# A graph layer on one core: VectorE adds messages and squares for two groups in one instruction

## The chip, the core and the metric

The kernel runs on one core of a Trainium2 chip. A core has five engines with a queue each: TensorE (PE in the profile, with its weight loads as PEld), VectorE (DVE), ScalarE (ACT), GpSimd (POOL) and SyncE (SP), which here only issues DMAs. Engines run side by side and wait for each other by semaphores; each works through its own queue in order. SBUF is the working memory with 128 partitions, PSUM holds the results of TensorE in eight banks of 2 KB a partition.

The metric is the device time of one execution in microseconds (us). A change is judged by the median of several runs.

## The reference

A graph has 12,500 nodes with 96 features, 412,500 edges sorted by their end node `dst`, and 4 features an edge. Cut to what matters:

```python
def _mlp(h, W, b, gamma, beta):
    h = relu(h @ W + b)
    mu, var = mean(h, 0), mean(square(h - mu), 0)     # over all rows
    return gamma * (h - mu) * rsqrt(var + 1e-5) + beta

node = _mlp(x, W_node, b_node, ...)
edge = _mlp(edge_attr, W_edge, b_edge, ...)
message = concatenate([x[src], x[dst], edge], axis=1)  # 412500 x 288
message = _mlp(message, W_msg, b_msg, ...)
agg = segment_sum(message, dst, num_segments=12500)
out = layernorm(x + agg + node)
```

The message needs the sum and the sum of squares of relu(...) over all edges, so its normalisation is applied at the end, to the sums by node.

## The kernel before

`W_msg` has three parts, and so has the message before its relu. The part of `x[src]` is computed once for all nodes into a table in HBM (`p_tab`, function `tables`), and rows are fetched from there by edge. The part of `x[dst]` lies in a second table (`q_tab`); since edges are sorted by `dst`, a block of edges needs only a window of its rows. The part of the edge is computed anew by TensorE from the edge's features.

**Tiles.** 128 edges are a tile, 4 tiles a group (806 groups), 4 groups a block (202 blocks). The rows of `x[src]` for a group come by `gather` (L210): one indirect DMA of GpSimd for each tile. Groups of the first 29 blocks are gathered early, before their messages can be computed, and put into HBM (`spill`); the main loop gets them back with plain DMAs (`fetch`, tile `pb`). All other groups land in `ring`, which has room for 16 groups, two groups to a tile. In the main loop `ahead_of` issues the gathers of the group 16 places ahead.

**Tiles without a gather.** For some groups the last of the four tiles isn't gathered. `COPIED` (L85) lists 349 such groups: their 128 columns of the transposed `x`, which lies in SBUF as `big`, are copied one by one to a tile `xc` by ScalarE (one column an instruction, L676) or VectorE (two columns an instruction, L672, and one XOR in `mend`, L681, at the end), and TensorE multiplies them by the weights (L779). `LOADS` (L74) says how many columns each of the two copies in each of four successive steps. `BY_ROW` lists 36 groups whose last tile is fetched row by row by SyncE's DMAs.

**The main loop** (`fast`, L867) has one step for each group `k`, in an order of every engine written out by hand (`manual_schedule`). In a step:

- SyncE loads edge features, the window of `q_tab` and numbers for the copies (`load`, `fetch`, `listed`, `fetch_rows`).
- VectorE: a part of the column copies, then `message(k)` (L797): z in PSUM plus the gathered rows, clamped at 0 from below, into a half of `h`. Then more copies, and `moments` (L816): the square of a group, made by ScalarE, is added to `wide_sq`, which lies in the PSUM tile `mixed`. Once a block `places_of` (L805) compares `rel` with `nodes_of`, also in `mixed`, to make the matrix that says which edge belongs to which node, and `add` (L845, L846) adds the finished block's sums to `agg`.
- ScalarE: `squared` (L811) once for two groups, `prepare` (L766: relu of the edge part into `left`) once for two groups, and column copies.
- TensorE: `sums(k - 2)` (L826: sums by node), `linear(k + 2)` (L774, L779: edge part, `x[dst]` part and copied tiles into the next z), `edges` (L758).
- GpSimd: the gathers of a group, always 16 groups ahead.

z has three banks (`ZB` = 3), `h` three tiles of two groups, `left` two tiles of a block, and the PSUM tile `pr` of two banks is used for `edges` and for products that nobody reads (`unread`, L634), which stand at the end between the last sums.

**The end.** After the last group, the last moments, sums and `add`s give mean and variance. `output` (L1103) forms the matrix `d` from them (L1111 to L1118, with two more unread products, L1121), multiplies it with `agg` for 98 tiles of 128 nodes (L1129), and for each eight of these adds the rest (L1135), squares and sums (L1139 or L1141 and L1142), takes root and reciprocal, scales (L1146) and stores. In `output`, groups of eight tiles with odd number are squared by eight ScalarE instructions that also sum, the others by one ScalarE instruction and a sum on VectorE. `general`, for inputs whose windows don't fit, isn't run.

Of the kernel before, what the change touches and what calls it, by code (L numbers as in the profile page):

```python
# [13 lines left out]
F32 = mybir.dt.float32  # L14
# [52 lines left out]
AB, HP, RB, ZB = 2, 3, 3, 3  # L67
# [6 lines left out]
LOADS = (((24,), (28,)) * 2, ((16, 16),) * 4)  # L74
AHEAD_BY = 18
LP = (NG - SPILL) // 2
BUSY = 5
# [7 lines left out]
COPIED = sorted([*range(RING + 1, 2 * (LP - 6), 2), *range(RING + 32, 2 * (LP - 8), 36)])  # L85
# [29 lines left out]
def gnn(ctx, tc, t):  # L115
# [396 lines left out]
    def fast():  # L512
# [49 lines left out]
        with tc.tile_pool(name="fix", bufs=1) as fix, tc.tile_pool(name="msg", bufs=2) as work, \  # L562
# [22 lines left out]
            left = [fix.tile([P, BG, GE], F32, name=f"left{i}") for i in range(2)]  # L585
# [12 lines left out]
            zb = [ps.tile([P, GE], F32, name=f"z{i}", bufs=1) for i in range(ZB)]  # L598

            eas, block, prs, windows = {}, {}, {}, {}  # L600
# [22 lines left out]
            def fetch(s):  # L623
                b = order[s]
                if b * BG < SPILL:
                    back = work.tile([P, BG, GT, C], F32, name="pb", bufs=1)
                    nc.sync.dma_start(back, spill[b].rearrange("p g (a c) -> p g a c", a=GT))
                    for i in range(BG):
                        got[b * BG + i] = back[:, i, :, :]

            def unread(n):
                busy = ps.tile([P, 2, GE], F32, name="pr", bufs=1)[:, 0, :GE // 2]
                for i in range(n):
                    nc.tensor.matmul(busy, ident[:C], big[:C, -GE // 2:], start=True, stop=True)  # L634
# [9 lines left out]
            numbers = [fix.tile([1, TURN, P], I32, name=f"numbers{i}") for i in range(2)]  # L644
# [116 lines left out]
            def prepare(s, half):  # L761

                n = min(2, NG - order[s] * BG - 2 * half)
                if n > 0:
                    pr, x = prs.pop((s, half)), left[s % 2]
                    nc.scalar.activation(x[:, 2 * half:2 * half + n, :], pr[:, :n, :], AF.Relu)  # L766

            def linear(k):
# [4 lines left out]
                for i in range(n):  # L773
                    nc.tensor.matmul(zb[k % ZB][:, i * C:(i + 1) * C],  # L774
                                     left[s % 2][:KR, g % BG, i * P:(i + 1) * P],
# [12 lines left out]
            def message(k):  # L788
                s, g = steps[k]
                n = min(GT, NT - g * GT)  # L790
                z = zb[k % ZB][:, :n * C].rearrange("p (t c) -> p t c", c=C)
                h = hb[k // 2 % HP][:, k % 2, :, :C]
                rows = got.pop(g)
# [3 lines left out]
                nc.vector._custom_dve(TENSOR_ADD_SAT, out=h[:, :n, :], in0=z, in1=rows[:, :n, :],  # L797
# [422 lines left out]
```

## Time and profile before

| | |
|---|---|
| median of 3 runs | 3613.63 us (3613.0 to 3615.57) |
| the profiled execution | 3611.83 us, of which the span from first to last instruction is 3610.1 us |
| mean granted TensorE clock | 0.771 of full speed |
| first message (L795/L797) | at about 612 us of the span |
| last gather begins | at 3545.8 us of the span |
| output products (L1129) | 3557.6 to 3599.8 us |
| VectorE, `moments` | 804 instructions, 444.3 us |
| ScalarE, column copies | 19968 instructions, 1932.9 us |

Times in the views count from the start of the span. A group of instructions is told as: line, engine, operation, out<-in, shapes, count | busy us, mean ns of one | idle time of the engine just before them, and what ended it. Instructions of one engine can overlap at their ends, so busy time divided by count can be less than the mean of one. "issue" is time in which an engine waited for nothing that the profile shows. PEld is TensorE's loading of weights beside its products (PE). Every fp32 product stands in the profile as two instructions.

### The profile page before, as it was taken

The page shows a single profiled execution, that of the slowest core. Times are in us where ns is not written, and L with a number is a line of the kernel's source. Part 1 is how long each engine was busy: PE and PEld are TensorE (multiplying, and loading weights), DVE is VectorE, ACT ScalarE, POOL GpSimd, SP SyncE. Part 2 cuts the span into 40 slices and gives each one's busy share as a digit, 9 for nine tenths or more (in the row PEclk, how much of TensorE's full clock was granted, in tenths as well). Part 3 has the DMA queues.
Part 4 walks back from the last instruction along what each step waited for, and adds up shares of the span by engine and source line. Part 5 has one row for each costly group of instructions (what it writes and reads, how often), then busy time and mean ns, then how long its engine had stood idle before and what let it go on. Part 6 is the DMA issues. An engine that isn't in the chain of part 4 may idle for free. (4 is left out here: it accounts for less than half of the span.)

```text
span 3610.1 us, 90270 instructions
## 1 busy us (share of the span) xinstructions
PE 2588.0 (72%) x15924; PEld 2197.9 (61%) x16147; DVE 3133.6 (87%) x15669; ACT 2989.8 (83%) x21332; POOL 2693.5 (75%) x2853
## 2 busy tenths in 40 slices
PE   4766765787877777776777777767777677777667
PEld 4313412676766666666666666666667566667667
DVE  3798798898988999998999999898999989999843
ACT  1687687788999999888998898899898989889832
POOL 7777777777777777777777777777777777777774
PEclk7766667888788778787877778787887978777875
DMA  9676664222222222222222222222222222222232
GB/s 254 168 199 190 178 191 110 59 64 63 59 64 63 63 60 53 63 63 62 59 65 63 62 64 59 62 64 63 59 64 62 58 60 59 62 63 63 62 99 68
DMA packets 219742, 303.63 MB, mean 84 GB/s; under 512 B 130416, under 2 KB 145894, under 8 KB 219026
## 3 DMA queue, kind: packets, MB, share of 16 engines
q0 software_dynamic: 90720, 139.53, 18.9%
q1 hardware_dynamic: 115474, 153.30, 14.2%
q10 hardware_dynamic: 12960, 4.93, 0.5%
q14 instruction: 459, 3.76, 0.3%
q8 instruction: 129, 2.11, 0.2%
HBM read 241.43 MB, written 56.09 MB: 82 GB/s over the span
## 5 line engine op out<-in xcount | busy, mean ns | idle before, releaser
L215 POOL DMA_INDIRECT pg<-p_tab,src x2771 | 2615.8, 944 | 847.8 <-issue 699.6
L676 ACT ACTIVATE xc<-big 96x1 f32 x19968 | 1932.9, 187 | 116.5 <-issue 102.2
L672 DVE SCALAR_TENSOR_TENSOR xc<-first_of_two,big 96x2 int32<-96x2 int32 x12352 | 1758.1, 209 | 107.8 <-issue 95.4
L774 PE MATMUL z<-rhs,left 128*128 128x96 f32 x6446 | 1137.9, 331 | 649.8 <-DVE h L797 637.5
L774 PEld LDWEIGHTS z<-rhs,left 128*128 128x128 f32 x6446 | 1004.7, 237 | 742.3 <-DVE h L797 729.9
L826 PEld LDWEIGHTS pa<-at,h 128*97 128x97 f32 x6446 | 833.4, 206 | 106.8 <-issue 40.1
L826 PE MATMUL pa<-at,h 128*97 128x80 f32 x6446 | 847.9, 287 | 20.4 <-issue 9.9
L797 DVE CUSTOM_DVE_ANT_0 h<-z,pg 128x384 f32<-128x384 f32 x690 | 377.1, 546 | 198.6 <-DMA pg<-p_tab,src 196.8
L811 ACT ACTIVATE sq<-h 128x768 f32<-128x768 f32 x404 | 335.2, 830 | 212.5 <-DVE mixed L816 204.6
L816 DVE TENSOR_TENSOR mixed<-mixed,sq 128x384 f32<-128x384 f32 x804 | 444.3, 553 | 0.4
L766 ACT ACTIVATE left<-pr 128x1024 f32<-128x1024 f32 x403 | 403.7, 1002 | 35.1 <-PE pr L758 25.1
L446 ACT ACTIVATE r<-pr 128x1024 f32<-128x1024 f32 x303 | 304.0, 1025 | 87.5 <-DVE estats L448 36.7
L448 DVE BATCH_NORM_STATS2 estats<-r 128x6 f32<-128x512 f32 x606 | 363.8, 677 | 8.5 <-ACT r L446 8.5
L442 PE MATMUL pr<-ea,wide 128*128 128x512 bf16 x587 | 249.6, 522 | 118.3 <-ACT r L446 117.8
L758 PE MATMUL pr<-late,we 128*128 128x512 bf16 x515 | 213.0, 474 | 89.1 <-DMA late<-stack 43.4
L442 PEld LDWEIGHTS <-wide 128*128 128x128 bf16 x606 | 71.1, 118 | 279.2 <-issue 265.0
L758 PEld LDWEIGHTS <-we 128*128 128x128 bf16 x806 | 101.4, 132 | 122.6 <-issue 100.9
L779 PE MATMUL z<-w_msg,xc 96*128 96x96 f32 x698 | 157.4, 313 | 0.0
L805 DVE TENSOR_TENSOR at<-rel,mixed 128x496 f32<-128x496 bf16 x202 | 132.0, 653 | 0.0
L779 PEld LDWEIGHTS z<-w_msg,xc 96*128 96x128 f32 x698 | 127.9, 228 | 0.0
L215 POOL DMA_INDIRECT pg<-in_x,src_raw x64 | 60.7, 949 | 20.8 <-issue 19.2
L410 PE MATMUL pn<-scaled,agg 96*128 96x96 f32 x196 | 52.4, 362 | 21.3 <-DVE y0s L413 21.3
(153 smaller groups left out, 1005.9 us busy)
## 6 DMA issues: line engine op xcount, KB each, us to landing
row<-p_tab SPq DMA_DIRECT2D x4608, 0.4 KB
pg<-p_tab,src POOLq DMA_INDIRECT x2771
pb<-spill SPq DMA_DIRECT2D x29, 768.0 KB
spill<-pg SPq DMA_DIRECT2D x55, 384.0 KB
ea<-stack SPq DMA_DIRECT2D x28, 420.0 KB
stack<-y SPq DMA_DIRECT2D x48, 224.0 KB
late<-stack SPq DMA_DIRECT2D x53, 180.0 KB
rhs<-q_tab SPq DMA_DIRECT2D x202, 46.5 KB
```

Source lines behind the costliest of these rows:

```text
L215: made = [nc.gpsimd.indirect_dma_start(out=pg[:, i, :], out_offset=None, in_=tab[:, :], in_offset=bass.IndirectOffsetOnAxis(ap=idx[:, i:i ...
L442: nc.tensor.matmul(pr[:, k % 2, :], wide[:, P * i:P * (i + 1)], ea[:, b % J, :], start=True, stop=True)
L448: nc.vector.bn_stats(stats[:, (k - o) % NS, (k - o) // NS, :], r[:, 1 - o, :])
L672: nc.vector.scalar_tensor_tensor(to[:, lo + i:lo + i + 2], first_of_two, a, b.to_broadcast([C, 2]), op0=OP.bitwise_and, op1=OP.bitwise_xor)
L676: nc.scalar.activation(to[:, lo + i:lo + i + 1], x.bitcast(F32), AF.Copy)
L758: nc.tensor.matmul(prs[s, half][:, i, :], we[:, 2 * half + i, :], block[s], start=True, stop=True)
L766: nc.scalar.activation(x[:, 2 * half:2 * half + n, :], pr[:, :n, :], AF.Relu)
L774: nc.tensor.matmul(zb[k % ZB][:, i * C:(i + 1) * C], left[s % 2][:KR, g % BG, i * P:(i + 1) * P], rhs[:KR, s % RB, g % BG, :], start=True, ...
L797: nc.vector._custom_dve(TENSOR_ADD_SAT, out=h[:, :n, :], in0=z, in1=rows[:, :n, :], s0=MOST, s1=0.0)
L811: nc.scalar.activation(sq[:, :m, :n, :], hb[k // 2 % HP][:, k % 2:k % 2 + m, :n, :C], AF.Square)
L816: nc.vector.tensor_tensor(wide_sq, wide_sq, sq[:, i, :, :], op=OP.add)
L826: nc.tensor.matmul(by_place[s % 2][:C + 1, :NW], hb[k // 2 % HP][:r, k % 2, t, :], at[s % AB][:r, i, o + NW * t:o + NW * (t + 1)], start=i ...
```

## The change

- `ZB` is 4. z lies in two PSUM tiles of two banks each, and `message` handles two groups in one instruction, in even steps; `linear` works three steps ahead.
- `wide_sq` has room for two groups and lies in SBUF; `moments` adds the squares of both groups in one instruction, in odd steps, from the square made in the step before it (`now`; it was one pair older). `nodes_of` is the SBUF tile `iota`. The PSUM tile `mixed` is gone. `places_of` of the next block comes in the third step of a block instead of the fourth.
- `left` has three tiles of half a block instead of two of a block. `numbers` lies in a partition of `big` that held nothing.
- `COPIED` has 366 groups, 17 more; `LOADS` changes from 104 + 128 columns in four steps (ScalarE + VectorE) to 108 + 136.
- `unread` multiplies bf16 tiles (`we`, `rel`) with 512 columns instead of fp32 with 256; there are four such products at each of the three places at the end (before: 4, 3 and 3), and three in each of the last seven steps where no `edges` product is waiting in `pr`.
- `output`: TensorE's order is by hand, the two unread products are bf16 with 512 columns, and eight single squares are used for every third set of tiles (i % 3 == 1) instead of every second.

```diff
-AB, HP, RB, ZB = 2, 3, 3, 3
+AB, HP, RB, ZB = 2, 3, 3, 4
...
-LOADS = (((24,), (28,)) * 2, ((16, 16),) * 4)
+LOADS = (((28,), (24,), (28,), (28,)), ((16, 16), (16, 20)) * 2)
...
-BUSY = 5
+BUSY, WARM, DENSE = 4, 7, 3
...
-COPIED = sorted([*range(RING + 1, 2 * (LP - 6), 2), *range(RING + 32, 2 * (LP - 8), 36)])
+COPIED = sorted([*range(RING + 1, 2 * (LP - 6), 2), *range(RING + 32, 2 * (LP - 8), 18)])
...
-            mixed = ps.tile([P, GE], F32, name="mixed", bufs=1)
-            wide_sq = mixed[:, :GT * C].rearrange("p (t c) -> p t c", c=C)
+            wide_sq = fix.tile([P, 2, GT, C], F32, name="wide_sq")
...
-            nodes_of = mixed[:, GT * C:GT * C + BG * WN].rearrange("p (k w) -> p k w", w=WN)
-            nc.vector.tensor_copy(nodes_of, iota)
+            nodes_of = iota
...
-            left = [fix.tile([P, BG, GE], F32, name=f"left{i}") for i in range(2)]
+            left = [fix.tile([P, 2, GE], F32, name=f"left{i}") for i in range(3)]
...
-            zb = [ps.tile([P, GE], F32, name=f"z{i}", bufs=1) for i in range(ZB)]
+            zp = [ps.tile([P, 2, GE], F32, name=f"z{i}", bufs=1) for i in range(ZB // 2)]
+            zb = [zp[i // 2][:, i % 2, :] for i in range(ZB)]
...
             def unread(n):
-                busy = ps.tile([P, 2, GE], F32, name="pr", bufs=1)[:, 0, :GE // 2]
+                busy = ps.tile([P, 2, GE], F32, name="pr", bufs=1)[:, 0, :]
                 for i in range(n):
-                    nc.tensor.matmul(busy, ident[:C], big[:C, -GE // 2:], start=True, stop=True)
+                    nc.tensor.matmul(busy, we[:, i % BG, :], rel.rearrange("p g t -> p (g t)")[:, :GE], start=True, stop=True)
...
-            numbers = [fix.tile([1, TURN, P], I32, name=f"numbers{i}") for i in range(2)]
+            numbers = [big[C:C + 1, i * TURN * P:(i + 1) * TURN * P].bitcast(I32).rearrange("o (k e) -> o k e", k=TURN) for i in range(2)]
...
-            def message(k):
+            def message(k, m=2):
+
                 s, g = steps[k]
                 n = min(GT, NT - g * GT)
-                z = zb[k % ZB][:, :n * C].rearrange("p (t c) -> p t c", c=C)
-                h = hb[k // 2 % HP][:, k % 2, :, :C]
-                rows = got.pop(g)
+                i = k % 2
+                z = zp[k // 2 % 2][:, i:i + m, :n * C].rearrange("p g (t c) -> p g t c", c=C)
+                h = hb[k // 2 % HP][:, i:i + m, :n, :C]
...
-                nc.vector._custom_dve(TENSOR_ADD_SAT, out=h[:, :n, :], in0=z, in1=rows[:, :n, :],
-                                      s0=MOST, s1=0.0)
+                rows = backs[s][:, g % BG - i:] if g < SPILL else ring[(g - SPILL) % RING // 2]
+                nc.vector._custom_dve(TENSOR_ADD_SAT, out=h, in0=z, in1=rows[:, i:i + m, :n, :], s0=MOST, s1=0.0)
...
-            def moments(sq, i):
-
-                nc.vector.tensor_tensor(wide_sq, wide_sq, sq[:, i, :, :], op=OP.add)
+            def moments(sq, m=2):
+
+                nc.vector.tensor_tensor(wide_sq[:, :m], wide_sq[:, :m], sq[:, :m], op=OP.add)
...
-                    message(k)
+                    if k % 2 == 0:
+                        message(k)
                     j = k - LATER - BG - 1
                     if k % 2 == 0 and k >= 2:
-                        now, before = squared(k - 2), now
+                        now = squared(k - 2)
                         acts.load()
-                    if g % BG == 3 and s + 1 < len(order):
+                    if g % BG == 2 and s + 1 < len(order):
                         places_of(s + 1)
                     dves.load()
                     dves.copy()
-                    if k >= 4:
-                        moments(before, k % 2)
+                    if k % 2 and now is not None:
+                        moments(now)
...
+                    if k >= last - WARM and not prs:
+                        unread(DENSE)
                     acts.copy()
...
-                unread(BUSY - 1)
+                unread(BUSY)
...
-                unread(BUSY - 2)
+                unread(BUSY)
...
-                if i % 2:
+                if i % 3 == 1:
                     for g in range(n):
                         nc.scalar.activation(sq[:, g, :], y[:, g, :], AF.Square, accum_out=sd[:, g:g + 1])
```

More of the change, by code (lines that the diff above doesn't have):

```diff
@@ L627, in fetch @@
                     nc.sync.dma_start(back, spill[b].rearrange("p g (a c) -> p g a c", a=GT))
+                    backs[s] = back
                     for i in range(BG):
@@ L764, in prepare @@
                 if n > 0:
-                    pr, x = prs.pop((s, half)), left[s % 2]
-                    nc.scalar.activation(x[:, 2 * half:2 * half + n, :], pr[:, :n, :], AF.Relu)
+                    pr, x = prs.pop((s, half)), left[(2 * s + half) % 3]
+                    nc.scalar.activation(x[:, :n, :], pr[:, :n, :], AF.Relu)
             def linear(k):
@@ L865, in fast @@
                 places_of(0)
-                now, before, last = None, None, BG * (len(order) - 1)
+                now, last = None, BG * (len(order) - 1)
                 for k in range(last):
@@ L896, in fast @@
                         linear(k + ZB - 1)
+                    if k % 2 == 0 and k + ZB < n and order[steps[k + ZB][0]] < RAW:
+                        transposed(k + ZB)
                     u = g % BG
@@ L903, in fast @@
                         edges(s + 1 + u // 2, (u // 2 + 1) % 2)
-                    if k % 2 and k + ZB < n and order[steps[k + ZB][0]] < RAW:
-                        transposed(k + ZB)
                     if g >= SPILL:
@@ L915, in fast @@
                 m, r = NT - (g + 1) * GT, E - (NT - 1) * P
-                waiting = squared(last - 2)
-                for x in (now, waiting):
-                    for i in range(2):
-                        moments(x, i)
-                message(last)
+                moments(squared(last - 2))
+                nc.vector.tensor_tensor(wide_sq[:, 0], wide_sq[:, 0], wide_sq[:, 1], op=OP.add)
+                message(last, 1)
                 sq = squared(last, 1, GT)
@@ L1110, in output @@
             a_m = scaled[:, C:C + 1]
-            nc.scalar.activation(sd, mstat[:, 1:2], AF.Sqrt, bias=eps[:C], scale=scale)
-            nc.vector.tensor_scalar(less, center, mstat[:, 0:1], -1.0, op0=OP.mult, op1=OP.mult)
-            nc.vector.reciprocal(sd, sd)
-            nc.vector.tensor_mul(a_m, sd, v["g_msg"])
-            nc.vector.tensor_scalar(d[:C], center, a_m, None, op0=OP.mult)
-            nc.tensor.matmul(pd, shift, center, start=True, stop=False)
-            nc.tensor.matmul(pd, scaled, less, start=False, stop=True)
-            nc.scalar.activation(d[C:C + 1], pd[C:C + 1], AF.Copy)
-            busy = ps.tile([P, GE // 2], F32, name="busy", bufs=1)
-            for i in range(2):
-                nc.tensor.matmul(busy, ident[:C], big[:C, -GE // 2:], start=True, stop=True)
+            with tc.manual_schedule(engines={ET.PE}):
+                nc.tensor.matmul(pd, shift, center, start=True, stop=False)
+                nc.scalar.activation(sd, mstat[:, 1:2], AF.Sqrt, bias=eps[:C], scale=scale)
+                nc.vector.tensor_scalar(less, center, mstat[:, 0:1], -1.0, op0=OP.mult, op1=OP.mult)
+                nc.vector.reciprocal(sd, sd)
+                nc.vector.tensor_mul(a_m, sd, v["g_msg"])
+                nc.vector.tensor_scalar(d[:C], center, a_m, None, op0=OP.mult)
+                busy = ps.tile([P, GE], F32, name="busy", bufs=1)
+                nc.tensor.matmul(pd, scaled, less, start=False, stop=True)
+                for i in range(2):
+                    nc.tensor.matmul(busy, we[:, i, :], rel.rearrange("p g t -> p (g t)")[:, :GE], start=True, stop=True)
+                nc.scalar.activation(d[C:C + 1], pd[C:C + 1], AF.Copy)
             out = t["out"].rearrange("(b p) f -> p b f", p=P)
```

14 lines of the change are left out of this document (7 added, 7 removed).

## The prediction

> **What bounds the kernel now.** The first line of the page comes first. VectorE (DVE) has the largest share, so the reader's first guess is that VectorE sets the time.
>
> ```profile
> PE 2588.0 (72%) x15924; PEld 2197.9 (61%) x16147; DVE 3133.6 (87%) x15669; ACT 2989.8 (83%) x21332; POOL 2693.5 (75%) x2853
> ```
>
> The table by stage (stretch, busy us and instruction counts of PE, PEld, DVE, ACT and POOL, then granted clock) says otherwise.
>
> ```profile
> 300.00:600.00 300.00, 194.17 (x635) 88.83 (x646) 267.58 (x450) 227.96 (x236) 226.79 (x241) 0.67 0.63 173
> 1500.00:1800.00 300.00, 216.36 (x1482) 197.08 (x1503) 276.34 (x1571) 269.54 (x2201) 226.73 (x241) 0.78 0.27 61
> 3000.00:3300.00 300.00, 225.59 (x1469) 205.35 (x1488) 277.27 (x1580) 270.22 (x2207) 226.79 (x241) 0.78 0.27 61
> ```
>
> The other engines change their load from stage to stage, but POOL issues 241 gathers in every 300 us, in stages with quite different work. The view of the gather's line gives count, durations and times, and the view of waits says what held POOL and what held the messages:
>
> ```profile
> L215 POOL DMA_INDIRECT pg<-p_tab,src x2771: 940/944/1100, 83.5 to 3545.8; - x198
> L215 POOL DMA_INDIRECT pg<-in_x,src_raw x64: 940/944/1123, 3.2 to 82.2; - x64
> ...
> POOL pg L215 <- issue: 718.8, 2357, 0.3
> DVE h L797 <- DMA pg<-p_tab,src: 196.8, 118, 5.1
> ```
>
> 2771 + 64 = 2835 gathers start between 3.2 and 3545.8 us, so one starts every 3542.6 / 2834 = **1.250 us**: 0.944 busy and a pause that is never longer than 0.3. POOL never stops for a free ring slot, while VectorE's messages stop 118 times for a gather, up to 5.1 us. The gathers pace the kernel from its third microsecond to 3546; VectorE's 87% is not the bound. After the last gather comes a serial end, read from the chain of work that ended last (start, us):
>
> ```profile
> 3542.04 2.51 DMA pg<-p_tab,src
> ...
> 3547.57 2.77 PE pr L634 x6
> 3550.34 0.95 PE pa L826 x6
> 3551.29 0.84 PE mixed L938 x6
> 3552.13 2.77 PE pr L634 x6
> 3554.90 0.32 PE pd L1116 x2
> 3555.22 1.76 PE busy L1121 x4
> 3556.98 0.34 PE pd L1117 x2
> ...
> 3557.64 41.29 PE py L1129 x192
> 3598.95 0.97 DVE y L1135
> ```
>
> So the time is 2835 gathers, about 11 us from the last gather to the output products, 42 us of those, and about 11 us of last rows and stores (3599 to 3610).
>
> **The change part by part.** The sum is made against the profiled run: 3611.83 us, of which the span is 3610.1. The median shown is 1.8 above it.
>
> *Seventeen gathers less.* `COPIED` grows from 349 to 366, and every copied tile is a gather that POOL does not issue: 17 x 1.250 = **21.2 us**, provided that VectorE and ScalarE stay faster than POOL. Two stretches of three blocks (12 messages) show how fast they are when no message waits:
>
> ```profile
> 1267.60:1307.10 39.50, 6.51 (x12) 0.80 0.26 57
> ...
> 1267.60:1307.10 39.50, 28.39 (x195) 25.89 (x196) 39.48 (x229) 37.61 (x312) 29.86 (x32) 0.80 0.26 57
> 1371.10:1410.80 39.70, 27.76 (x213) 25.13 (x216) 39.57 (x230) 38.61 (x316) 29.94 (x33) 0.91 0.25 55
> ```
>
> A block of four steps takes 13.2 us there, with VectorE busy 100% and ScalarE 95 to 97%. POOL gives such a block, on average over the 202 blocks, 2374 gathers x 1.25 / 202 = 14.7 us before and 2357 x 1.25 / 202 = 14.6 after. The engines have 1.4 us a block to spare.
>
> *Copies.* `LOADS` goes from 104 + 128 columns in four steps to 108 + 136.
>
> ```profile
> L676 ACT ACTIVATE xc<-big 96x1 f32 x19968 | 1932.9, 187 | 116.5 <-issue 102.2
> L672 DVE SCALAR_TENSOR_TENSOR xc<-first_of_two,big 96x2 int32<-96x2 int32 x12352 | 1758.1, 209 | 107.8 <-issue 95.4
> ```
>
> Instructions overlap, so I divide busy time by count: 97 ns a column on ScalarE, 142 ns for two on VectorE. A block gains 4 x 0.097 = 0.4 us on ScalarE and 4 x 0.142 = 0.6 on VectorE; in all, six tiles (768 columns, 74 us) and eleven tiles (704 instructions, 100 us).
>
> *Two groups at once.* Messages and moments go from two instructions of 384 elements to one of 768.
>
> ```profile
> L797 DVE CUSTOM_DVE_ANT_0 h<-z,pg 128x384 f32<-128x384 f32 x690 | 377.1, 546 | 198.6 <-DMA pg<-p_tab,src 196.8
> L816 DVE TENSOR_TENSOR mixed<-mixed,sq 128x384 f32<-128x384 f32 x804 | 444.3, 553 | 0.4
> ...
> L1135 DVE TENSOR_TENSOR y<-py,big 128x768 f32<-128x768 f32 x12 | 11.5, 958 | 27.9 <-PE py L1129 25.5 <-POOL y L1146 2.4
> L1146 DVE TENSOR_TENSOR y<-y,sd 128x768 f32<-128x768 f32 x1 | 1.0, 959 | 0.0
> ```
>
> L1135 has the new message's form (two PSUM banks plus SBUF) and L1146 the new moment's (SBUF alone): 0.96 us instead of 1.1, so about 0.13 each, four in a block: 0.5 us. Where instructions overlap at their ends the gain is smaller, at worst half. VectorE's block thus ends between 13.2 + 0.1 and 13.2 + 0.4, and ScalarE's at 12.7 + 0.4 = 13.1. I take 13.5 us against POOL's 14.6: nothing of VectorE's or ScalarE's new work shows, and nothing of their gain either. This cover is worth 1.1 x 202 = 220 us.
>
> *New waits.* A message now waits for both groups' gathers, and behind it in VectorE's queue stand the copies, and behind those PE's linear products of the next pair. It costs nothing as long as two steps of VectorE (6.7 us) fit into two groups of gathers (7.3). Four banks give PE four steps of room instead of three. The moment now waits for the square of the pair in front of it, one step old instead of two to three: that is the first rival. `left` as three halves, `numbers` in rows of `big` that the copies don't read, and the earlier `places_of` move work by a step inside engines that have room; each 0, at most one stall of about 1 us a block, which the same 1.1 us covers. Seventeen more `memset`s of some 0.14 us likewise. The last two messages stay single, so the end starts as before.
>
> *The end.* Row L634 x6 shows three fp32 dummy products of 256 columns at 2.77 us. The new ones are bf16 with 512 columns, four each time. Two and one such products at half clock and at full clock, and eight linear products at each:
>
> ```profile
> 3455.33 2.02 PE L774 MATMUL z<-rhs,left 128*128 128x96 f32 x8 [0.53 <-DVE h L797]
> 3460.96 1.06 PE L758 MATMUL pr<-late,we 128*128 128x512 bf16 x2
> 3467.64 1.13 PE L774 MATMUL z<-rhs,left 128*128 128x96 f32 x8 [2.71 <-DVE h L797]
> 3468.61 0.38 PE L758 MATMUL pr<-late,we 128*128 128x512 bf16 x1
> 3473.84 0.59 PE L758 MATMUL pr<-late,we 128*128 128x512 bf16 x2
> ```
>
> 0.59 - 0.38 gives 0.21 us a product at full clock, and twice that, 0.43, at half. Four cost 1.7 or 0.85 instead of 2.77, and in `output` two cost 0.85 or 0.43 instead of 1.76. Of the three places the first gives about 0.5 (the message of the last group is then the later one), the other two 1 and 0.9: with half clock 2.5 us, with full clock 3.5. Moving i = 11 from eight ScalarE squares (2.2 us) to one (0.84) and a VectorE sum ends the last rows 0.7 earlier.
>
> *The clock of the output products.* Here is the second large term. 196 instructions take 42.1 us, 0.215 each; eight linear products of the same 96 columns take 2.02 at half clock and 1.13 at full, so at full clock 196 would take 196 x 0.141 = 27.7. The granted clock (third number from the end) in stretches of 3.41 us, the spacing at which it changes:
>
> ```profile
> 3456.02:3459.43 3.41, 3.32 (x18) 3.11 (x18) 0.90 (x2) 0.00 (x0) 2.72 (x3) 0.50 0.42 120
> 3459.43:3462.85 3.42, 3.42 (x17) 3.00 (x18) 1.17 (x3) 1.63 (x2) 2.59 (x3) 0.51 0.84 273
> ...
> 3459.43:3462.85 3.42, 1.06 (x2) 0.35 (x2) 0.51 0.84 273
> ...
> 3572.04:3575.45 3.41, 3.41 (x17) 3.41 (x17) 0.95 (x2) 1.17 (x8) 0.00 (x0) 0.50 0.42 116
> ```
>
> The first stretch, fp32 only, was followed by another at half clock; the second, with two bf16 products, by one at full clock (the linear products of 3467.64 ran in it); the third, inside the output products, has PE busy throughout and stays at half. An estimate over all 484 half-clock stretches of the trace, 151 of them followed by full clock, with one unit for a bf16 column and two for an fp32 column (times the share of rows used): about 3050 units lift the clock. The output products make 2400, the old dummies some 2800; four bf16 products make 2048 in 1.7 us, and with the sums beside them some 3300. At full clock about 2250 (fp32 at 1.5) hold it, and the output products would then make 2600: once lifted they hold it themselves. The 18 products of the last seven steps (six of them pass `not prs`) and the twelve behind them do this if a stretch ends well against them. Laying the stretches at 24 positions over my sequence of PE's last 40 us, a little over half reach the output products at full clock, a few in their first stretch. I take full clock, and 13 us of the 14.4, since the other engines then have little room: POOL's product 1.47, ScalarE about 2.05 with every third tile in single squares, against PE's 2.26 a tile.
>
> The Trainium skill (TensorE: Matmul & The Clock Gate, Part 1: The HAM clock gate) says that about 3.4 us of busy TensorE release the full clock. Its window length agrees with the 3.41 us here; the release does not, since the output products stay at 0.50 through 42 us of busy PE. By that rule the clock of the output would not depend on the dummies, and the sum would be that of the half-clock rival.
>
> Sum: 21.2 + 3.5 + 0.7 + 13 = 38.4, so 3573.4 in a run like the profiled one, 3575.2 beside the median; rounded, **3576**.
>
> **The rivals.**
> *Half clock remains* (the dense products don't do what they are there for): 21.2 + 2.5 + 0.7 = 24.4, so 3589 beside the median. For it: the position of the stretches is not set by the kernel, and nearly half of the positions fail. Against it: the count of units above.
>
> *VectorE waits for ScalarE's square* (slower than before). The moment follows its square by one step, and the square stands on ScalarE behind 27 copies (27 x 0.097 = 2.6 us). If each pair waits 0.83, the time of a square, a block takes 13.5 + 1.7 = 15.2, and the engines take over from POOL: 0.6 x some 190 copying blocks = 114, in place of a gain of 38: 3690. It decides from 14.6 - 13.5 = 1.1 us a block, 0.55 a pair; it is slower than before from about 0.65 a pair. Against it: ScalarE may run ahead, since a square needs a message of two steps ago, and it has 3 to 5% left.
>
> *Longer gathers.* The moment and `places_of` now read SBUF alone. In the trace, POOL beside such instructions of VectorE (start, us):
>
> ```profile
> 73.29 0.96 POOL L215 DMA_INDIRECT pg<-in_x,src_raw  x1 [0.30 <-issue]
> 73.92 0.56 DVE L281 TENSOR_TENSOR whole<-whole,part 128x384 f32<-128x384 f32 x1
> ...
> 88.45 1.10 POOL L215 DMA_INDIRECT pg<-p_tab,src  x1 [0.30 <-issue]
> 88.88 0.21 DVE L294 TENSOR_SCALAR lins<-lins 39x128 int32<-39x128 int32 x1
> ```
>
> Beside the all-SBUF add the gather has 0.96, beside the two `tensor_scalar`s of L294 and L298 1.10. Priced at 0.16 each, 403 moments and 202 `places_of` give +97 and 3673; at 0.016, +10 and 3586. The 12352 copies of L672, also of two SBUF inputs, stand beside gathers whose median stays 944 ns; I expect 0. The Trainium skill (SBUF — State Buffer, Who interferes with whom) says that a VectorE instruction with two SBUF inputs contends with a GpSimd instruction that reads SBUF; this is that rule's case, and L281 and L672 speak against a price here.
>
> **How the numbers follow.** Forecast 0.51 (own range 3572 to 3581); half clock 0.36 (3586 to 3592); both slower rivals together 0.07; gain of the gathers partly eaten (0.1 to 0.5 us a block, 3593 to 3630) 0.06. The range 3571 to 3593 holds the first two. A measurement of this kernel tells about 0.2%, 7 us, from no change: faster 0.90, same 0.03, slower 0.07.
>
> **What would show it.** 2818 gathers, still 1.250 us apart, the last about 21 us earlier; message waits still ended by gathers; messages and moments near 0.96; output products at clock 1.00 and 0.14 an instruction. Wrong would be: POOL pauses over 0.3, moments waiting for squares, gathers over 0.95, or output products at 0.215.

## The result, and the profile after

The changed kernel takes **3829.57 us** (median of 4 runs, 3820.86 to 3840.98). The kernel before, run beside it, takes 3613.68 (4 runs, 3613.0 to 3615.57). The ratio is 1.0598 [1.0566, 1.0631]: 6% slower, where 3576 was forecast.

The page of the profile after shows the changed groups (count | busy us, mean ns of one | idle before):

```profile
PE 2580.2 (68%) x15963; PEld 2240.5 (59%) x16189; DVE 3200.8 (84%) x15599; ACT 3089.6 (81%) x22070; POOL 2923.6 (76%) x2836
...
L215 POOL DMA_INDIRECT pg<-p_tab,src x2754 | 2846.0, 1033 | 846.9 <-issue 790.3
...
L799 DVE CUSTOM_DVE_ANT_0 h<-z,pg 128x768 f32<-128x768 f32 x346 | 327.3, 946 | 282.4 <-DMA pg<-p_tab,src 211.4
...
L817 DVE TENSOR_TENSOR wide_sq<-wide_sq,sq 128x768 f32<-128x768 f32 x403 | 380.6, 944 | 0.7 <-ACT sq L812 0.7
```

Three things are to be read here. VectorE's two new instructions have the lengths that were forecast (946 and 944 ns). The moments (L817) wait 0.7 us for ScalarE's squares in the whole run, so the first slower rival did not come true. But the mean gather (L215) takes 1033 ns instead of 944, and messages now wait 211 us for gathers instead of 197. POOL is still the pace, and it became slower. Its pauses between gathers still end at 0.3 us, but for one stop of 7.5 us at 190 us, before the main loop, which waits for `spill` (the view of waits: us in total, times, longest):

```profile
POOL pg L215 <- issue: 809.5, 2655, 0.3
...
POOL pg L215 <- DMA spill<-pg: 7.8, 2, 7.5
```

The table by stage shows the same from the other side:

```profile
300.00:600.00 300.00, 197.92 (x647) 90.34 (x658) 266.64 (x437) 227.67 (x235) 226.56 (x241) 0.68 0.64 175
1500.00:1800.00 300.00, 201.04 (x1361) 187.67 (x1381) 260.25 (x1433) 260.67 (x2130) 232.61 (x222) 0.80 0.25 57
```

Before the main loop POOL still issues 241 gathers in 300 us. In the main loop, where the pairs are added, it issues 222 and is nevertheless busy for longer (232.6 us instead of 226.7). The gathers' own line, and that of the output products:

```profile
L215 POOL DMA_INDIRECT pg<-p_tab,src x2754: 940/944/2227, 83.3 to 3775.0; - x197
...
L1132 PE MATMUL py<-dm,agg x196: 275/275/421, 3783.6 to 3806.2; 97*128 97x96 f32 x196
```

The three durations are the shortest, the median and the longest. The median gather is untouched at 944 ns, but the longest lasts 2227 where 1100 was the longest before. So some gathers are held and most are not. Counted over the trace: 428 gathers last more than 1.0 us, and what they last beyond 0.944 adds up to **246.7 us**. Before, 7 gathers and 0.8 us. Of the 246.7 us, 235.0 lie in 381 gathers that run beside a moment (L817) and 11.5 in 45 beside `places_of` (L806).

The balance of the two profiled spans, 3822.0 - 3610.1 = +211.9 us:

| | us |
|---|---|
| gathers held longer | +246 |
| 17 gathers fewer, as forecast | -21.2 |
| rest up to the last gather (3545.8 to 3775.0 is +229.2) | +4.5 |
| last gather to the output products (11.9 to 8.6) | -3.2 |
| output products (42.1 to 22.8) | -19.3 |
| last product to the end of the span (10.3 to 15.5) | +5.2 |

The rest of 4.5 us is that stop for `spill`, which takes 3.0 us in the kernel before.

Two places of the timeline after show what happens to a gather (start, length, engine; only the lines of the gathers and of the moment):

```profile
1504.16 0.95 POOL L215 DMA_INDIRECT pg<-p_tab,src  x1 [0.30 <-issue]
1504.93 0.94 DVE L817 TENSOR_TENSOR wide_sq<-wide_sq,sq 128x768 f32<-128x768 f32 x1
1505.42 1.27 POOL L215 DMA_INDIRECT pg<-p_tab,src  x1 [0.31 <-issue]
...
1513.24 0.94 POOL L215 DMA_INDIRECT pg<-p_tab,src  x1 [0.30 <-issue]
1514.48 2.00 POOL L215 DMA_INDIRECT pg<-p_tab,src  x1 [0.30 <-issue]
1514.72 0.95 DVE L817 TENSOR_TENSOR wide_sq<-wide_sq,sq 128x768 f32<-128x768 f32 x1
1516.79 0.94 POOL L215 DMA_INDIRECT pg<-p_tab,src  x1 [0.31 <-DVE xc L672]
```

The moment of 1504.93 starts 0.77 us into a gather, and that gather keeps its 0.95. It still runs when the next gather starts at 1505.42; that one lasts 1.27 and ends 0.82 after the moment. The moment of 1514.72 starts 0.24 us into a gather, and this gather lasts 2.00 and ends 0.81 after the moment. It looks as if a gather had to get through its first part without such an instruction beside it, and as if 0.82 us remained once it is over.

### The profile page after: what moved, and what is told of

It reads as the page before. It is cut to its first block, busy times and chain, and to the rows that moved or that the text cites. A ratio compares the mean times of both kernels' runs of the same rounds, so it can differ in the third digit from the quotient of the medians.

```text
span 3822.0 us, 90369 instructions
## 1 busy us (share of the span) xinstructions
PE 2580.2 (68%) x15963; PEld 2240.5 (59%) x16189; DVE 3200.8 (84%) x15599; ACT 3089.6 (81%) x22070; POOL 2923.6 (76%) x2836
## 5 line engine op out<-in xcount | busy, mean ns | idle before, releaser
L215 POOL DMA_INDIRECT pg<-p_tab,src x2754 | 2846.0, 1033 | 846.9 <-issue 790.3
L676 ACT ACTIVATE xc<-big 96x1 f32 x20736 | 2005.8, 188 | 200.5 <-issue 174.5
L672 DVE SCALAR_TENSOR_TENSOR xc<-first_of_two,big 96x2 int32<-96x2 int32 x13056 | 1843.2, 210 | 168.4 <-issue 156.8
L774 PE MATMUL z<-rhs,left 128*128 128x96 f32 x6446 | 1214.9, 348 | 943.6 <-DVE h L799 933.4
L774 PEld LDWEIGHTS z<-rhs,left 128*128 128x128 f32 x6446 | 1095.6, 255 | 997.7 <-DVE h L799 986.1
L827 PE MATMUL pa<-at,h 128*97 128x80 f32 x6446 | 830.2, 283 | 22.1 <-issue 6.5
L799 DVE CUSTOM_DVE_ANT_0 h<-z,pg 128x768 f32<-128x768 f32 x346 | 327.3, 946 | 282.4 <-DMA pg<-p_tab,src 211.4
L817 DVE TENSOR_TENSOR wide_sq<-wide_sq,sq 128x768 f32<-128x768 f32 x403 | 380.6, 944 | 0.7 <-ACT sq L812 0.7
L779 PE MATMUL z<-w_msg,xc 96*128 96x96 f32 x732 | 173.5, 326 | 0.0
L806 DVE TENSOR_TENSOR at<-rel,iota 128x496 f32<-128x496 bf16 x202 | 133.1, 659 | 1.2 <-PE pa L827 1.2
L215 POOL DMA_INDIRECT pg<-in_x,src_raw x64 | 60.7, 949 | 20.7 <-issue 19.2
```

The costliest lines, as they stand in the source:

```text
L215: made = [nc.gpsimd.indirect_dma_start(out=pg[:, i, :], out_offset=None, in_=tab[:, :], in_offset=bass.IndirectOffsetOnAxis(ap=idx[:, i:i ...
L672: nc.vector.scalar_tensor_tensor(to[:, lo + i:lo + i + 2], first_of_two, a, b.to_broadcast([C, 2]), op0=OP.bitwise_and, op1=OP.bitwise_xor)
L676: nc.scalar.activation(to[:, lo + i:lo + i + 1], x.bitcast(F32), AF.Copy)
L774: nc.tensor.matmul(zb[k % ZB][:, i * C:(i + 1) * C], left[(2 * s + g % BG // 2) % 3][:KR, g % 2, i * P:(i + 1) * P], rhs[:KR, s % RB, g % ...
L779: nc.tensor.matmul(zb[k % ZB][:, i * C:(i + 1) * C], xcs[copied_at[g - SPILL] % XB], w_msg[:, 0, :], start=False, stop=True)
L799: nc.vector._custom_dve(TENSOR_ADD_SAT, out=h, in0=z, in1=rows[:, i:i + m, :n, :], s0=MOST, s1=0.0)
```

## The experiments

The theory after this reading: **a VectorE instruction that reads two SBUF operands holds a gather's beginning**; the moments and `places_of` read one operand from PSUM before, and none after. Rivals: it is not the operands but the length of 768 elements, or the pairing of the steps; or the denser work of some other part (more copies, the new end) is to blame. The first four runs take the change apart.

**No moments.** The changed kernel without them:

```diff
-                    if k % 2 and now is not None:
-                        moments(now)
```

> The changed kernel without its 402 moments in the loop (the sum of squares is left out, all else stays). Theory: a gather that begins while VectorE runs a long add with both inputs in SBUF stands still until that add ends; of the 247 us by which gathers over 1.0 us exceed 0.944, all but about 12 lie beside L817. Then gathers are 0.944 again, and the time is 3613.7 - 21.2 (17 gathers) - 17 (end) + 12 (places_of from SBUF) = about 3588 us. Rival: the pairs themselves (messages that wait for two groups, PE behind them, ScalarE with more copies) make the loop slow: then it stays over 3700.

Measured: 3623.46 us (one run; before beside it 3611.96). The last gather starts at 3574.7 instead of 3775.0:

```profile
L215 POOL DMA_INDIRECT pg<-p_tab,src x2754: 940/944/1893, 83.7 to 3574.7; - x197
```

The 200 us belong to the moments, then, but not all that is lost: 115 gathers are still held, 48.8 us in all, of which 110 with 47.8 us stand beside `places_of`. That instruction held 11.5 us in the kernel after; without the moments it falls at other places against the gathers and holds four times as much.

**The same moment with one operand from PSUM.** A moment at the same place, of the same length, that reads z instead of the sum:

```diff
-                        moments(now)
+                        z = zp[k // 2 % 2][:, :, :GT * C].rearrange("p g (t c) -> p g t c", c=C)
+                        nc.vector.tensor_tensor(wide_sq, z, now, op=OP.add)
```

> The changed kernel with the moment's instruction as long as before and written to the same SBUF tile, but with one input from PSUM (z of the pair instead of the running sum, so the sum of squares is not computed). Theory (two SBUF inputs hold the gather): gathers beside L817 stay at 0.944, about 3588 us; a little more if the z banks, now read a second time, come free too late. Rival (any VectorE instruction of 0.95 us at this place, or its writing to SBUF, holds the gather): about 3825 us, as the changed kernel.

Measured: 3636.76 us (one run). The gathers' line, and the output products', which ran at half clock in this run (41.6 us; about 20 of the 3636 are theirs):

```profile
L215 POOL DMA_INDIRECT pg<-p_tab,src x2754: 940/944/1882, 83.5 to 3572.8; - x197
...
L1133 PE MATMUL py<-dm,agg x196: 365/421/422, 3581.3 to 3622.9; 97*128 97x96 f32 x196
```

A moment now starts well inside the sensitive part of a gather, and nothing happens to the gather (only the lines of the gathers and of the moment):

```profile
1525.47 0.94 POOL L215 DMA_INDIRECT pg<-p_tab,src  x1 [0.30 <-issue]
1525.71 0.94 DVE L893 TENSOR_TENSOR wide_sq<-z,sq 128x768 f32<-128x768 f32 x1
1526.72 0.94 POOL L215 DMA_INDIRECT pg<-p_tab,src  x1 [0.30 <-issue]
```

This one is 0.24 us in, as far as the one of 1514.72 above, whose gather lasted 2.00; a count over the whole trace says it better than one place. It asks when the VectorE instruction starts, counted from a gather's start, and how long that gather lasts beyond 0.944 (number of cases, mean us). The first column has the gathers that start while the instruction runs; the other two sort all instructions by the last gather that started before them:

```
                                  running at the    starts 0 to 0.35   starts later
                                  gather's start    after it
after, L817  (two SBUF, 0.94)     310   +0.481      92    +0.929       311   +0.001
e2,    L893  (one PSUM, 0.94)     309   +0.000      92    +0.003       309   +0.004
```

The instructions have the same length, the same place and nearly the same number in each column. Only the operand differs. This settles the length and the pairing as rivals: what is left of e2's loss, 46.8 us, is again nearly all (44.6) beside `places_of`. The result is written to the same SBUF tile in both kernels, so the place of the output isn't the cause either.

**The parts that are no pair.** The kernel before with the 366 copied groups, the new `LOADS` and the new end, but with messages and moments of single groups and sums in PSUM (the diff's core; the end as in the change):

```diff
-LOADS = (((24,), (28,)) * 2, ((16, 16),) * 4)
+LOADS = (((28,), (24,), (28,), (28,)), ((16, 16), (16, 20)) * 2)
...
-COPIED = sorted([*range(RING + 1, 2 * (LP - 6), 2), *range(RING + 32, 2 * (LP - 8), 36)])
+COPIED = sorted([*range(RING + 1, 2 * (LP - 6), 2), *range(RING + 32, 2 * (LP - 8), 18)])
```

> The kernel before with the 17 more copied groups, the new LOADS and the new end (dense unread products, order of output), without pairs and with the running sum in PSUM. Theory: the gathers stay the pace and the pairs are not needed for it: 3613.7 - 21.2 - 17 = 3576 us. Rival (VectorE, which needs 13.2 + 0.6 us a block, and ScalarE with 13.1, become the bound without the pairs): 3600 or more.

Measured: 3575.05 us (4 runs: three from 3572.0 to 3575.45, one 3588.49), ratio 0.9906 [0.9884, 0.9929]. Gathers' line, then the waits:

```profile
L215 POOL DMA_INDIRECT pg<-p_tab,src x2754: 940/944/1040, 83.8 to 3526.9; - x197
```

```profile
DVE h L797 <- DMA pg<-p_tab,src: 115.6, 64, 5.6
```

The last gather starts 18.9 us earlier than before, and messages still wait for gathers. The forecast's whole sum stands here, 3576 against 3575, without the pairs. More copies and the new end are not to blame.

**Pairs with both sums back in PSUM.** To have room for that, I took one of the two banks of `by_place`, and `add` comes one step earlier (the diff's core):

```diff
-            by_place = [ps.tile([P, GE], F32, name=f"pa{i}", bufs=1) for i in range(2)]
+            by_place = [ps.tile([P, GE], F32, name="pa", bufs=1)] * 2
...
-            wide_sq = fix.tile([P, 2, GT, C], F32, name="wide_sq")
+            mixed = ps.tile([P, GE], F32, name="mixed", bufs=1)
+            wide_sq = mixed[:, :GT * C].rearrange("p (t c) -> p t c", c=C)
...
-                nc.vector.tensor_tensor(wide_sq[:, :m], wide_sq[:, :m], sq[:, :m], op=OP.add)
+                for i in range(m):
+                    nc.vector.tensor_tensor(wide_sq, wide_sq, sq[:, i], op=OP.add)
```

> The changed kernel with messages in pairs and four z banks, but with the running sum and nodes_of in PSUM as before (moments of one group each; the two banks of the sums by node become one to make room, and add comes one step earlier). It computes everything. Theory: no gather is held, 3613.7 - 21.2 - 17 = 3576 us. Rival (the pairs are the cause): over 3700.

A miss: 4027.52 us, ratio 1.1154 [1.1135, 1.1172]. The waits show why:

```profile
PE pa L830 <- DVE agg L850: 1229.5, 195, 9.1
...
POOL pg L215 <- DVE h L801: 472.3, 73, 19.1
```

With one bank, PE waits 195 times for VectorE's `add` before it may start the next block's sums; messages fall behind, and POOL for the first time stands before a full ring. Only 5 gathers last more than 1.0 us, but a kernel that is bound by something else can't say what the pairs cost.

**One sum alone in SBUF.** The second round goes the other way: the kernel before, and only `wide_sq` (e5) or only `nodes_of` (e6) moved to SBUF. In e5 `numbers` also moves into `big`, as in the change, to make room.

```diff
-            wide_sq = mixed[:, :GT * C].rearrange("p (t c) -> p t c", c=C)
+            wide_sq = fix.tile([P, GT, C], F32, name="wide_sq")
```

> The kernel before with one thing changed: the running sum of squares lies in SBUF (804 adds of one group, 0.55 us each; the numbers lie in big, to make room). Theory: gathers that begin during such an add wait for its end. From the changed kernel's trace: an add of 0.95 holds a gather by what is left of it, and a gather in its first 0.3 us too, 0.58 us on average; an add of 0.55 by about 0.2, 804 of them +150 us (90 to 200), about 3765 us. Rival (only the pairs make it slow): 3614.

```diff
-            nodes_of = mixed[:, GT * C:GT * C + BG * WN].rearrange("p (k w) -> p k w", w=WN)
-            nc.vector.tensor_copy(nodes_of, iota)
+            nodes_of = iota
```

> The kernel before with one thing changed: places_of reads nodes_of from SBUF (202 instructions of 0.65 us with two SBUF inputs). Theory: in the changed kernel 12 us of held gathers lie beside it, since most of them begin right behind a message that has just waited for a gather; here +5 to +25, about 3625 us. Rival (bf16 and fp32 inputs do not hold gathers): 3614.

Measured: e5 3848.32 us (one run; before 3613.25), +235. e6 3684.64, ratio 1.0187 [1.0147, 1.0227], +71. Each of the two moves alone is a loss, and both are larger than expected. The gathers' lines of e5 and of e6:

```profile
L215 POOL DMA_INDIRECT pg<-p_tab,src x2771: 942/947/1773, 84.0 to 3781.9; - x198
```

```profile
L215 POOL DMA_INDIRECT pg<-p_tab,src x2771: 942/947/1822, 83.8 to 3625.2; - x198
```

511 gathers are held in e5, 229.9 us; 137 in e6, 71.9 us (71.2 of them beside `places_of`). The count by place, as above:

```
                                  running at the    starts 0 to 0.35   starts later
                                  gather's start    after it
before, L816 (one PSUM, 0.55)     368   0.000       188   0.000        616   0.000
e5,     L816 (two SBUF, 0.55)     290   +0.171      311   +0.578       493   +0.012
e6,     L804 (two SBUF, 0.65)      90   +0.208       82   +0.643       120   +0.002
```

Nothing of the pairing is in these two kernels, so a second operand in SBUF is enough.

**Does a gather get in between two short adds?** The changed kernel with each moment as two instructions of 384 elements:

```diff
-                nc.vector.tensor_tensor(wide_sq[:, :m], wide_sq[:, :m], sq[:, :m], op=OP.add)
+                for i in range(m):
+                    nc.vector.tensor_tensor(wide_sq[:, i], wide_sq[:, i], sq[:, i], op=OP.add)
```

> The changed kernel with each moment as two adds of one group, one right behind the other, still in SBUF. Theory, if a gather gets in between two VectorE instructions: it waits for the end of one add only, and the holding falls from 235 us to about 150 to 190 (as 804 adds by themselves): about 3750. If it does not get in between, the pair holds 1.1 us together: 3830 or more.

Measured: 3842.34 us (one run), 429 gathers held, 265.2 us, the longest 2257 ns. Two adds back to back hold a gather like one long one; it doesn't get in between: of 216 gathers that start beside the first add, 200 end 0.82 us after the second add and one 0.82 us after the first.

**The end alone.** The kernel before with the new `unread` products and `output`:

> The kernel before with the new end only (dense bf16 unread products, order and squares of output). Theory: the output products run at full clock, 3613.7 - 17 = 3597 us, with single executions near 3611 if the clock's stretches fall badly. Rival (the end gained in the changed kernel for another reason, its pairs): 3611 to 3614.

Measured: 3598.49 us (10 runs), ratio 0.9971 [0.9955, 0.9987]. Seven runs lie between 3594.2 and 3599.5, three between 3610.6 and 3611.2. The profiled one is of the first kind:

```profile
L1132 PE MATMUL py<-dm,agg x196: 247/275/350, 3558.6 to 3580.6; 97*128 97x96 f32 x196
```

196 products take 22 us instead of 42. The other nine runs have no profile; that the three longer ones kept half clock is read from their 14 us alone, and e2 above shows such an execution of the new end. So the new end lifts the clock of the output in most runs and fails in some, near the forecast's chances (0.51 to 0.36). Which of its parts does it (the dense products or the order of `output`) wasn't tried apart, and one of the 13 runs of the kernel before took 3596.64.

**What the pairs are worth without the loss.** The changed kernel with a PSUM operand in both instructions: the moments as in e2, and `places_of` with a bank of z in place of `nodes_of`:

```diff
-                    nodes_of[:, :m].unsqueeze(2).to_broadcast([P, m, GT, WN]), op=OP.is_equal)
+                    zp[1][:, 0, :m * WN].rearrange("p (k w) -> p k w", w=WN).unsqueeze(2).to_broadcast([P, m, GT, WN]), op=OP.is_equal)
```

It computes neither the sum of squares nor the sums by node. It was run four times, as e9, e11, e13 and e15:

> The changed kernel with its pairs, its four z banks, 366 copied tiles and its end, but the moment and places_of each take one input from PSUM (z instead of the running sum and of nodes_of; so neither the sum of squares nor the sums by node are right), at the same lengths and places. Theory: no gather is held any more, 1.250 us apart, 3613.7 - 21.2 - 17 = 3576 us; the z banks are read twice, which may cost up to 15. Rival (the pairs cost something of their own, since without the moments 3623 were measured): 3600 or more, with gathers of 0.944.

> The same kernel as e9, again, since in that run the kernel before took 5222 us instead of 3613 and the two can't be laid beside the others. Pairs, four z banks, 366 copied tiles and the new end as in the change, but moment and places_of with one input from PSUM (sum of squares and sums by node are not right). Theory: 3576 us, up to 15 more for z banks read twice, gathers 1.250 us apart. Rival (the pairs cost something of their own): 3600 or more, with gathers of 0.944.

> The kernel of e9 and e11 once more (pairs, four z banks, 366 copied tiles, new end; moment and places_of with one input from PSUM, sum of squares and sums by node not right). Theory: 3576 us, up to 15 more for z banks read twice, gathers 1.250 us apart. Rival (the pairs cost something of their own): 3600 or more, with gathers of 0.944.

> The kernel of e9, e11 and e13 once more. Theory: 3576 us, up to 15 more for z banks read twice, gathers 1.250 us apart. Rival (the pairs cost something of their own): 3600 or more, with gathers of 0.944.

**More copied tiles without pairs.** Kernel e4 with 384 copied groups:

```diff
-LOADS = (((28,), (24,), (28,), (28,)), ((16, 16), (16, 20)) * 2)
+LOADS = (((28,),) * 4, ((16, 20),) * 4)
...
-COPIED = sorted([*range(RING + 1, 2 * (LP - 6), 2), *range(RING + 32, 2 * (LP - 8), 18)])
+COPIED = sorted([*range(RING + 1, 2 * (LP - 6), 2), *range(RING + 32, 2 * (LP - 8), 12)])
```

This was run beside it each time, as e10, e12, e14 and e16:

> As the kernel before with the new copies and end, but 384 copied tiles (35 more than before, LOADS 112 + 144). If the gathers still set the pace: 3613.7 - 35 x 1.25 - 17 = 3553 us. If VectorE takes over (13.2 + 8 x 0.142 = 14.3 us a block against 2339 x 1.25 / 202 = 14.5 of the gathers, with the copying blocks nearer to the limit than the mean): 3560 to 3600.

> The same kernel as e10, again, for the same reason: the kernel before with 384 copied tiles, LOADS of 112 + 144 and the new end. If the gathers still set the pace: 3613.7 - 35 x 1.25 - 17 = 3553 us. If VectorE takes over: 3560 to 3600.

> The kernel of e10 and e12 once more (the kernel before with 384 copied tiles, LOADS of 112 + 144 and the new end). If the gathers still set the pace: 3553 us. If VectorE takes over: 3560 to 3600.

> The kernel of e10, e12 and e14 once more. If the gathers still set the pace: 3553 us. If VectorE takes over: 3560 to 3600.

In the first three rounds the kernel before itself took 5212 to 5222 us (e9 5729, e11 5731, e13 5725 and 5910; e10 5229, e12 5227, e14 5222), so those six can't be compared with the others; why is open. In them the gathers don't set the pace: in e9 POOL stands 1828.6 us before a full ring and ScalarE's copies wait 1609.4 us for issue (98.2 in e16). Beside the kernel before in the same rounds, e9 and e11 are about 10% slower (1.0957 and 1.0985) and e10, e12 and e14 level (1.0011 to 1.0016). Hardly a gather was held (1 us at most), so this loss is another, of a kernel in which TensorE also waits for the moment that reads z (1048.1 us in e9); it is left open. The fourth round: e15 3582.23 us (5 runs, 3575.96 to 3598.94; before 3620.37, 6 runs), ratio 0.9914 [0.9875, 0.9953]. e16 **3560.09 us** (3559.46 and 3560.72), ratio 0.9854 [0.9781, 0.9927]. The gathers of e15, then the gathers and the waits of e16 (POOL's pauses first):

```profile
L215 POOL DMA_INDIRECT pg<-p_tab,src x2754: 938/944/1497, 83.7 to 3527.5; - x197
```

```profile
L215 POOL DMA_INDIRECT pg<-p_tab,src x2736: 941/947/1182, 84.2 to 3512.7; - x196
```

```profile
POOL pg L215 <- issue: 658.4, 2158, 0.3
...
DVE h L797 <- DMA pg<-p_tab,src: 9.8, 6, 3.6
```

In e15 the last gather starts at 3527.5, against 3526.9 in e4: once no gather is held, and while gathers set the pace, the pairs cost nothing and bring nothing up to there. Undisturbed steps show no shorter block either: over stretches of three blocks in which VectorE never stops for 0.6 us, the median block takes 14.1 us in e15 (165 stretches) and 13.9 in e4 (343). e16 computes everything and is faster than both kernels of the change. There messages wait only 9.8 us for gathers (196.8 before), so VectorE and the gathers are about level, and there is little room for more copied tiles. The gathers still set the pace. Most of what lies between the 3553 expected for that and 3560 is their length: 947 ns in the median instead of 944, which is 8.2 us over 2736 gathers.

The gathers of the kernels paced by them, in one table (start of the last gather; what gathers over 1.0 us last beyond 0.944, and their count, with the 64 early ones of `in_x`):

| kernel | last gather at us | held us (gathers) | last minus held |
|---|---|---|---|
| before | 3545.8 | 0.8 (7) | 3545.0 |
| after | 3775.0 | 246.7 (428) | 3528.3 |
| e1, no moments | 3574.7 | 48.8 (115) | 3525.9 |
| e2, moment with PSUM | 3572.8 | 46.8 (122) | 3526.0 |
| e4, no pairs | 3526.9 | 1.2 (10) | 3525.7 |
| e5, squares in SBUF | 3781.9 | 229.9 (511) | 3552.0 |
| e6, nodes in SBUF | 3625.2 | 71.9 (137) | 3553.3 |
| e8, two adds | 3794.6 | 265.2 (429) | 3529.4 |
| e15, both with PSUM | 3527.5 | 2.1 (15) | 3525.4 |

The last column of the six kernels with 366 copied groups lies between 3525.4 and 3529.4, and 3545.8 - 21.2 is 3524.6. The held gathers account for the loss up to the last gather. e5 and e6, with 349 copied groups, belong beside the 3545.0 of the kernel before; they lie 7 and 8 us above it, about what a median gather of 947 instead of 944 ns makes over 2771 gathers (8.3).

## Why the prediction was wrong

**The pace, and seventeen gathers less: right.** e4 and e15 start the last gather 18.9 and 18.3 us earlier, where 21.2 were forecast. One reading was wrong without weight: a pause "never longer than 0.3" overlooks a stop of 3.0 us for `spill` at 186 us.

**The cover: it was enough, but smaller than put.** The block with pairs was put at 13.5 us against POOL's 14.6. Undisturbed it takes 14.1 in e15, and 13.9 in e4 without pairs, so about 0.5 us a block were left instead of 1.1, and the 0.1 to 0.4 that the pairs should save VectorE can't be seen. The waits for gathers remained, and nothing of the pairs' gain showed in the time, as said.

**New waits: right.** 0.7 us at the moments for the squares; the rival at 3690 fell.

**The end: right in sum, wrong in its terms.** From the last gather to the end of the span it is 47.0 us instead of 64.3, so -17.3, where -17.2 was forecast. But the output products gave 19.3 instead of 13 (0.116 us each instead of 0.141 at full clock), and the rows behind them gave back 5.2 instead of gaining 0.7: that faster products leave the last sums, squares and stores more behind would fit, but no run separates it from the changed squares. The stretch at the output shows PE still busy throughout, with the other engines at two thirds or less (PE, PEld, DVE, ACT, POOL, then the clock):

```profile
3784.00:3806.00 22.00, 22.00 (x193) 21.89 (x193) 14.61 (x24) 13.78 (x63) 10.37 (x8) 0.98 0.41 108
```

**Longer gathers: this is the step that failed.** "The 12352 copies of L672, also of two SBUF inputs, stand beside gathers whose median stays 944 ns; I expect 0." The mechanism had been named, and its rival priced at 0.16 us for each instruction: +97. It measured 235.0 / 403 = 0.58 us a moment, and from 0.06 (after) to 0.35 (e6) for a `places_of`. Three things were wrong in how the rows were read.

First, the neighbours were compared by kind and not by place. The `L281` quoted there started 0.63 us into its gather (73.92 against 73.29), where the counts above show next to nothing. A row of before with the right place existed:

```profile
3444.59 0.21 DVE L681 TENSOR_TENSOR xc<-xc 96x64 int32<-96x64 int32 x1
3444.60 1.02 POOL L215 DMA_INDIRECT pg<-p_tab,src  x1 [0.30 <-issue]
```

An XOR of two SBUF operands runs as a gather starts, and the gather lasts 1.02 instead of 0.94. It isn't alone: of the 15 XORs of before that start up to 0.10 us ahead of a gather, 14 go with a gather that is longer, by 0.02 to 0.07. At 0.21 us the instruction is so short that hardly more can be seen.

Second, the median of the gathers was used as evidence. It stays at 944 in the kernel after as well, in which 246.7 us are lost: the median says nothing of one case in seven (428 of all 2818). The maximum, 1100 against 2227, does.

Third, the price was taken from short or badly placed instructions, and the 0.16 from the `tensor_scalar`s of L294 and L298, which read one tensor and not two. The counts of the kernel after give a rule that prices it: an instruction of length d (0.55 us or more here) holds a gather if it starts between d before the gather's start and 0.35 after it, and the gather then ends about 0.82 us after the instruction, if that is later than 0.944. For a moment that stretch is 0.94 + 0.35 = 1.29 us long, and a gather starts every 1.25, so each moment finds one (402 cases for 403 moments). Starts spread evenly over the stretch give a mean hold of about 0.53 us, so some 214 us for all moments, an estimate; 235 were measured. For e6's 0.65 us the same gives 80% of the instructions and 0.38 us each, some 61 us; 71.2 were measured. For e5 it gives some 195 us, where 229 were measured.

The rule isn't complete. For the `places_of` of the kernel after it gives the same 61 us, and 11.5 were measured: 139 of the 202 start 0.50 to 0.55 us ahead of a gather, too early to hold it for long (0.02 us each), and of the 11 that start in a gather's first 0.35 us, 10 hold nothing, where 76 of 82 do in e6. Nor does it hold for the short instructions of before: of the 48 XORs that start in a gather's first 0.35 us none stands beside a longer gather, and of the 3078 copies of L672 that start there 30 do, by at most 0.07. So the copies were no evidence against a price for the moments; what separates short from long is open.

The Trainium skill (SBUF — State Buffer, Who interferes with whom) says that two SBUF inputs of VectorE contend with a GpSimd instruction that reads SBUF, and that one SBUF input, outside the two-port modes, does not. Both halves agree with the counts: +0.48 and +0.93 us with two, 0.000 and +0.003 with one. The prediction set this rule aside because of L281 and L672; the runs say it decides. What the runs add is that only the gather's beginning is open to such an instruction, and that a gather which began up to 0.35 us earlier is held as well.

Open is also the gather of 1.10 us that the prediction shows beside L294 and L298: they start 0.43 and 0.56 us into it, where the counts for two SBUF operands show next to nothing.

What stays open is why the beginning. That the gather reads its indices from SBUF there, and does something else in the other 0.6 us, would fit, but is only argued; no run separated the two. Nor was a version tried that shifts the moments to a fixed place against the gathers.

## What to carry to other kernels

Where GpSimd's DMAs set the pace, keep one operand of every long VectorE instruction in PSUM, as far as this case goes; freeing a PSUM bank by moving a running sum and `nodes_of` to SBUF cost 6% here, and the bank bought nothing. When a trace is to show that two instructions don't disturb each other, look for a pair that stands at each offset, short against long, before writing 0, and look at the longest one rather than the median. A doubt about the engine that sets the pace is priced by its count times the worst case (here 403 times 1 us), even if the chance is small.

## What the runs showed that was not expected

A gather is open to VectorE's instructions of two SBUF operands only in its first 0.35 us or so. What holds it there costs more than the overlap: the gather ends 0.82 us after the instruction's end, nearly its whole length again (the median both of the 310 cases and of the 92 of the kernel after).

How much an instruction costs depends on what else runs: `places_of` holds 11.5 us in the kernel after, 47.8 without the moments and 71.2 in e6. Its places against the gathers differ from kernel to kernel; that the held gathers themselves shift the later ones is a likely reason, but not shown.

At full clock the 196 output products take 0.116 us each, less than the 0.141 of the eight linear products of the same 96 columns.
